# A selective-scan layer: scan rows reordered to (channel, state), state sums in four column groups of one PSUM bank, stores of ACT-made tiles issued from ACT's queue, and the first convolution tap moved to ACT

## The chip, the cores and the metric

The kernel runs on one core of one Trainium2 chip. The metric is the device time of one execution in microseconds (us). Times are medians of four runs (for the kernel before, of three when it was first profiled).

## The reference, cut to what matters

The layer takes x of shape (8, 384, 32, 32): eight images of 1024 tokens and 384 channels. In float32 throughout:

```python
xz = layernorm(t) @ in_proj_w.T ; xm, z = split(xz)          # 768 inner channels
xc = silu(causal_conv3(xm))                                   # three taps per channel
dt, B, C = split(xc @ x_proj_w.T) ; dt = softplus(dt @ dt_proj_w.T + b)
h[t] = exp(dt[t] * A) * h[t-1] + dt[t] * xc[t] * B[t]          # 768 channels x 16 states
y[t] = sum over the 16 states of h[t] * C[t]  +  xc[t] * D
t = gelu((y * silu(z)) @ out_proj_w.T @ mlp_w1.T + b) @ mlp_w2.T + b ; x = x + t
x = x + ffn(norm(x))                                           # two projections with binarised weights
```

The scan over 768 x 16 independent rows of 1024 tokens is the core. For each image it takes 96 tiles of 128 rows.

## The kernel before

A tile of 128 rows is 32 channels by 4 states. Its work is a ring over four engines: an exponential on ACT, a product on GpSimd, the scan and a product with C on DVE, and a sum over the states on TensorE (a matmul with a 128x32 matrix of zeros and ones, `fold`). The projections of the neighbouring images are woven between the tiles; the order on each engine is fixed when the program is built. In the profiles PE is TensorE (PEld its weight loads), DVE is VectorE, ACT is ScalarE, POOL is GpSimd, and SPq and ACTq are the queues from which SP and ACT issue transfers. The parts that matter:

```python
# rows of a tile are (state, channel): partition = state * 32 + channel
def quad_rows(first, q):                      # B or C rows: 4 states, each to 32 partitions
    src = rows[first + q * SQ : first + (q + 1) * SQ, :]
    nc.sync.dma_start(r, src.unsqueeze(1).to_broadcast([SQ, DQ, L]))      # 4 x 32 x 1024
def rep(d, j, name):                          # dt or dt*x: 32 channels, each to 4 states; 3 buffers
    src = d[j * DQ : (j + 1) * DQ, :]
    nc.sync.dma_start(r, src.unsqueeze(0).to_broadcast([SQ, DQ, L]))      # 4 x 32 x 1024
...
def sums(py, pair, q, hcs):                   # py: 128 x 1024, two banks
    for cols in HALVES:
        for jj, hc in zip(pair, hcs):
            nc.tensor.matmul(py[jj * DQ : (jj + 1) * DQ, cols], self.fold, hc[:, cols], ...)
...
for m in range(KD):                           # 6 times 128 channels
    py = ...; xr = (1 buffer) ; zr = (1 buffer)
    for p0 in (0, 2):                         # two tiles at a time
        dts, dtxs = two loads each
        for q in range(NQUAD):
            for i, jj in enumerate(pair):
                da = exp(dts[i] * a)                                      # ACT, into PSUM, 2 buffers
                u = dtxs[i] * b_q[q]                                      # GpSimd
                da = scan(da, u)                                          # DVE
                hc = da * c_q[q]                                          # DVE, 4 buffers
            # the pair's sums are given out one tile later
```

All loads and stores except the constants are issued from SP's queue. The program's PSUM tiles take eight banks: four for da, two for py and two for the projections.

Of the kernel before, what the change touches and what calls it, by code (L numbers as in the profile page):

```python
# [30 lines left out]
P = 128  # L31
# [13 lines left out]
NQUAD = NS // SQ  # L45
NJ = DI // DQ

NUM_GROUPS = 5
# [14 lines left out]
class Layer:  # L63
    def __init__(self, ctx, tc, a, out):
        self.tc, self.nc, self.a, self.out = tc, tc.nc, a, out

        def pool(name, bufs, **kw):
            return ctx.enter_context(tc.tile_pool(name=name, bufs=bufs, **kw))

        self.const = pool("const", 1)  # L70
        self.big = pool("big", 4)
        self.wk = pool("wk", 2)
        self.wt = pool("wt", 4)
        self.small = pool("small", 2)
        self.sc = pool("scan", 2)
        self.bc = pool("bc", 1)
        self.dram = pool("dram", 2, space=DRAM)
        self.dram1 = pool("dram1", 1, space=DRAM)
        self.ps_da = pool("ps_da", 2, space=PSUM)
        self.ps_y = pool("ps_y", 1, space=PSUM)  # L80
        self.ps = pool("ps", 2, space=PSUM)
        self.st = {}
        self.x_mid = [self.dram1.tile([C, L], F32, name=f"x_mid{b}") for b in range(NQ)]
        self.constants()
# [3 lines left out]
    def constants(self):  # L88
# [6 lines left out]
        self.fold = const.tile([P, DQ], F32, name="fold")  # L95
        nc.vector.tensor_add(self.fold, ident[:, :DQ], ident[:, DQ : 2 * DQ])
        for k in range(2, SQ):
            nc.vector.tensor_add(self.fold, self.fold, ident[:, k * DQ : (k + 1) * DQ])
        self.eps_m = const.tile([P, 1], F32, name="eps_m")
# [4 lines left out]
        def vec(name, k):  # L104
# [4 lines left out]
        self.ln_w, self.ln_b, self.mlp_b2 = vec("ln_w", KC), vec("ln_b", KC), vec("mlp_b2", KC)  # L109
        self.conv_b, self.dt_b, self.d_skip = (  # L110
            vec("conv_b", KD), vec("dt_proj_b", KD), vec("D", KD),
        )
        self.mlp_b1 = vec("mlp_b1", KH)
# [57 lines left out]
    def s1(self, b):  # L171
        nc, a = self.nc, self.a
        dt_d = self.dram.tile([DI, L], F32, tag="dt_d", name="dt_d")
        dtx_d = self.dram.tile([DI, L], F32, tag="dtx_d", name="dtx_d")
        xc_d = self.dram.tile([DI, L], F32, tag="xc_d", name="xc_d")
        z_d = self.dram.tile([DI, L], F32, tag="z_d", name="z_d")
        rows = self.dram.tile([2 * NS, L], F32, tag="rows", name="rows")
# [6 lines left out]
        for half, cols in enumerate(HALVES):  # L184
# [11 lines left out]
            for m in range(KD):  # L196
                pm = self.mm3(self.w_cols(a["in_proj_w"][m]), t, "p_in")
                xm = self.wk.tile([P, T + 2], F32, tag="xm", name="xm")
                nc.scalar.copy(xm[:, 2:], pm)  # L199
                if half == 0:  # L200
                    nc.gpsimd.memset(xm[:, :2], 0.0)
                    nc.gpsimd.tensor_copy(halo[:, m, :], xm[:, T:])
                else:
                    nc.gpsimd.tensor_copy(xm[:, :2], halo[:, m, :])
                nc.vector.tensor_scalar(
                    xc[:, m, :], xm[:, :T], self.conv_w[:, m, 0:1],
                    self.conv_b[:, m : m + 1], ALU.mult, ALU.add,
                )
                for j in (1, 2):
                    nc.vector.scalar_tensor_tensor(  # L210
                        xc[:, m, :], xm[:, j : j + T], self.conv_w[:, m, j : j + 1],
                        xc[:, m, :], ALU.mult, ALU.add,
                    )
                yield 3
# [6 lines left out]
            nc.scalar.activation(z, z, AF.Silu)  # L221
            nc.sync.dma_start(tiled(xc_d, cols), xc)
            nc.sync.dma_start(tiled(z_d, cols), z)

# [7 lines left out]
            nc.scalar.copy(dbc, p_dbc)  # L232
            nc.sync.dma_start(rows[:, cols], dbc[R:, :])
            yield 6
# [10 lines left out]
            nc.scalar.activation(dt, dt, AF.Softplus)  # L245
            nc.sync.dma_start(tiled(dt_d, cols), dt)
            for d in range(KD):
# [6 lines left out]
    def s2(self, b):  # L254
        nc, tc = self.nc, self.tc
        dt_d, dtx_d, xc_d, z_d, rows = self.st[b]
        yg_d = self.dram.tile([DI, L], F32, tag="yg_d", name="yg_d")
        self.st[b] += (yg_d,)

        def quad_rows(first, q):  # L260
            r = self.bc.tile([P, L], F32, tag=f"bc{first}_{q}", name=f"bc{first}_{q}")
            src = rows[first + q * SQ : first + (q + 1) * SQ, :]
            nc.sync.dma_start(r, src.unsqueeze(1).to_broadcast([SQ, DQ, L]))
            return r

        def rep(d, j, name):
            r = self.sc.tile([P, L], F32, tag=name, name=name, bufs=3)
            src = d[j * DQ : (j + 1) * DQ, :]
            nc.sync.dma_start(r, src.unsqueeze(0).to_broadcast([SQ, DQ, L]))
            return r  # L270
# [3 lines left out]

        def sums(py, pair, q, hcs):
            for cols in HALVES:
                for jj, hc in zip(pair, hcs):
                    nc.tensor.matmul(  # L278
                        py[jj * DQ : (jj + 1) * DQ, cols], self.fold, hc[:, cols],
                        start=(q == 0), stop=(q == NQUAD - 1),  # L280
                    )

        def gate(m, py, xr, zr):
# [3 lines left out]
            nc.gpsimd.tensor_mul(xr, xr, zr)  # L287
            nc.sync.dma_start(yg_d[m * P : (m + 1) * P, :], xr)

        for m in range(KD):  # L290
            py = self.ps_y.tile([P, L], F32, tag="y", name="py")
            xr = self.sc.tile([P, L], F32, tag="xr", name="xr", bufs=1)
            zr = self.sc.tile([P, L], F32, tag="zr", name="zr", bufs=1)
            for p0 in (0, 2):
                pair = (p0, p0 + 1)
                dts = [rep(dt_d, m * SQ + jj, "dt_r") for jj in pair]
                dtxs = [rep(dtx_d, m * SQ + jj, "dtx_r") for jj in pair]
                if p0 == 0:
                    nc.sync.dma_start(xr, xc_d[m * P : (m + 1) * P, :])
                    nc.sync.dma_start(zr, z_d[m * P : (m + 1) * P, :])  # L300
                for q in range(NQUAD):
                    if q not in b_q:
                        b_q[q] = quad_rows(0, q)
                        c_q[q] = quad_rows(NS, q)
                    hcs = []
                    for i, jj in enumerate(pair):
                        col = (m * SQ + jj) * NQUAD + q
                        da = self.ps_da.tile([P, L], F32, tag="da", name="da")
                        nc.scalar.activation(  # L309
                            da, dts[i], AF.Exp, scale=self.a_neg[:, col : col + 1]  # L310
                        )
                        u = self.sc.tile([P, L], F32, tag="u", name="u")
                        nc.gpsimd.tensor_mul(u, dtxs[i], b_q[q])  # L313
                        nc.vector.tensor_tensor_scan(da, da, u, 0.0, ALU.mult, ALU.add)  # L314
                        hc = self.sc.tile([P, L], F32, tag="hc", name="hc", bufs=4)
                        nc.vector.tensor_mul(hc, da, c_q[q])  # L316
                        hcs.append(hc)
                        yield
                        if i == 0:
                            for f in late:  # L320
                                f()
                            late.clear()
                    late.append(lambda py=py, pair=pair, q=q, hcs=hcs: sums(py, pair, q, hcs))
            late.append(lambda m=m, py=py, xr=xr, zr=zr: gate(m, py, xr, zr))
# [5 lines left out]
    def s3(self, b):  # L330
        nc, a = self.nc, self.a
        yg_d = self.st[b][5]
        to = self.x_mid[b] if b < NQ else self.out[b]
        for cols in HALVES:
            yg = self.big.tile([P, KD, T], F32, tag="big", name="yg")
            nc.sync.dma_start(yg, yg_d[:, cols].rearrange("(k p) l -> p k l", p=P))
            t2 = self.wk.tile([P, KC, T], F32, tag="t", name="t2")
# [104 lines left out]
    def f1(self, b):  # L442
# [11 lines left out]
        for m in range(KH):  # L454
            w = self.w_cols(self.w1_d[m])
            for h, cols in enumerate(HALVES):
# [5 lines left out]
                )  # L462
                nc.sync.dma_start(y1_d[m, :, cols], y)
                yield 3
# [111 lines left out]
def _laid_out(i):  # L576
# [14 lines left out]
    a = {"x": np.asarray(i["x"]).reshape(B, C, L)}  # L591
    for n in ("ln_w", "ln_b", "conv_w", "conv_b", "dt_proj_b", "D", "mlp_b1", "mlp_b2"):
        a[n] = cols(i[c + n])
    for n in ("x_proj_w", "dt_proj_w"):
        a[n] = np.asarray(i[c + n]).T
    for n in ("in_proj_w", "out_proj_w", "mlp_w1"):
        a[n] = blocks(i[c + n])
    w2 = blocks(i[c + "mlp_w2"])
    a["mlp_w2"] = w2.reshape(KC, P, 2, HK, P).swapaxes(1, 2)

    al = np.asarray(i[c + "A_log"]).reshape(NJ, DQ, NQUAD, SQ)
    a["A_log"] = al.transpose(3, 1, 0, 2).reshape(P, NJ * NQUAD)
    for n in ("W1", "W2"):
# [22 lines left out]
```

## Time and profile before

| | before |
|---|---|
| median, lowest, highest of three runs | 5466.58, 5451.86, 5474.68 us |
| PE busy | 3987.9 us, 73% |
| DVE, GpSimd, ACT busy | 62%, 39%, 35% |
| DMA busy, mean of 16 engines | 41.5% |

The chain is the work that ended last, followed back from the end of the run through what released each step; "issue" is time for which the profile shows no wait. Here are its shares of the whole span by engine (it was followed back over the last 54% only), then the groups of the scan ring and of the convolution taps: line, engine, operation, operands, count, then busy us and mean ns of one, then idle time before it.

```profile
PE 21%; DMA 15%; DVE 7%; issue 4%; POOL 3%; ACT 2%; SPq 0%; POOLq 0%; DVEq 0%; ACTq 0%
...
L313 POOL TENSOR_TENSOR u<-dtx_r,bc 128x1024 f32<-128x1024 f32 x768 | 1836.4, 2404 | 2665.5 <-DVE da L314 2211.3
L314 DVE TENSOR_TENSOR_SCAN da<-da,u 128x1024 f32<-128x1024 f32 x768 | 1733.7, 2286 | 684.4 <-ACT da L309 597.0
L316 DVE TENSOR_TENSOR hc<-da,bc 128x1024 f32<-128x1024 f32 x768 | 910.9, 1213 | 631.5 <-PE py L278 604.3
...
L210 DVE SCALAR_TENSOR_TENSOR xc<-xm,conv_w,xc 128x512 f32<-128x512 f32 x192 | 155.0, 821 | 1.9
...
L205 DVE TENSOR_SCALAR xc<-xm,conv_w,v_conv_b 128x512 f32<-128x512 f32 x96 | 113.9, 1186 | 52.7 <-ACT xm L199 51.8 <-POOL xm L204 0.4
```

Every member of the ring spends most of its idle time waiting for another member (DVE for ACT and PE, GpSimd for DVE).

### The profile page before, as it was taken

The numbers are of one execution on the slowest core, as the hardware profiler recorded it, in microseconds if no ns is written. First come the engines' busy times: TensorE is split into PE (matmuls) and PEld (weight loads), VectorE is DVE, ScalarE is ACT, GpSimd is POOL, SyncE is SP. The second block draws the span as 40 slices with busy tenths as digits, with TensorE's granted clock in tenths as the row PEclk, the third lists the DMA queues.
The fourth block names the chain that finished last, engine by engine and source line by source line (L and its number), as shares of the span: only waits on it lengthen the run. The fifth ranks groups of instructions, "written<-read, shape, count | busy, mean of one in ns | idle before, by whom it ended". The sixth has DMA issues, their size and how long they took to land.

```text
span 5473.1 us, 29744 instructions
## 1 busy us (share of the span) xinstructions
PE 3987.9 (73%) x9252; PEld 1397.9 (26%) x9252; DVE 3383.6 (62%) x2345; ACT 1919.2 (35%) x1921; POOL 2112.1 (39%) x1072
## 2 busy tenths in 40 slices
PE   8574478756878758878387884887758777658859
PEld 3110032212322213223032221322213223222314
DVE  2598766774575554775646665466664667547860
ACT  3343233432344224443233531344323353223422
POOL 0365434443343243442434434334243343335530
PEclk8786588877988879989698886998869988778979
DMA  4344344333434434445343443446334355334522
GB/s 158 139 158 151 117 142 136 130 126 131 133 134 161 151 119 130 139 141 168 126 141 108 150 144 112 129 130 196 122 113 146 114 179 149 108 128 145 161 96 89
DMA packets 314545, 745.49 MB, mean 136 GB/s; under 512 B 23804, under 2 KB 92924, under 8 KB 314388
## 3 DMA queue, kind: packets, MB, share of 16 engines
q1 hardware_dynamic: 311984, 743.26, 41.5%
q8 instruction: 74, 1.21, 0.1%
q14 instruction: 83, 0.68, 0.0%
q10 hardware_dynamic: 2404, 0.33, 0.0%
HBM read 560.01 MB, written 183.50 MB: 136 GB/s over the span
## 4 chain that ended last, share of the span: by engine, by line
PE 21%; DMA 15%; DVE 7%; issue 4%; POOL 3%; ACT 2%; SPq 0%; POOLq 0%; DVEq 0%; ACTq 0%
DMA dt_r<-dt_d 6%; PE p_h L143 5%; PE p_o L367 3%; DVE da L314 3%; PE py L278 3%; PE p_out L342 3%; PE p_y L489 2%; PE p_y L143 2%; POOL u L313 2%; DVE hc L316 2%; DMA w<-in_mlp_w 2%; PE p_z L143 1%; DMA y_d<-y 1%; DMA yg_d<-xr 1%; ACT da L309 1%
## 5 line engine op out<-in xcount | busy, mean ns | idle before, releaser
L313 POOL TENSOR_TENSOR u<-dtx_r,bc 128x1024 f32<-128x1024 f32 x768 | 1836.4, 2404 | 2665.5 <-DVE da L314 2211.3
L314 DVE TENSOR_TENSOR_SCAN da<-da,u 128x1024 f32<-128x1024 f32 x768 | 1733.7, 2286 | 684.4 <-ACT da L309 597.0
L278 PE MATMUL py<-hc,fold 128*32 128x512 f32 x3072 | 1047.1, 721 | 744.7 <-DVE hc L316 704.8
L309 ACT ACTIVATE da<-dt_r,a_neg 128x1024 f32<-128x1024 f32 x768 | 853.8, 1116 | 1949.5 <-DVE hc L316 1318.5
L316 DVE TENSOR_TENSOR hc<-da,bc 128x1024 f32<-128x1024 f32 x768 | 910.9, 1213 | 631.5 <-PE py L278 604.3
L143 PE MATMUL p_h<-t,w 128*128 128x512 f32 x1152 | 533.8, 619 | 110.2 <-DMA w<-in_mlp_w 73.5
L278 PEld LDWEIGHTS py<-hc,fold 128*32 128x32 f32 x3072 | 194.1, 120 | 1536.5 <-DVE hc L316 933.5
L367 PE MATMUL p_o<-g,w 128*128 128x512 f32 x1152 | 519.1, 606 | 17.2 <-DMA w<-in_mlp_w 16.2
L143 PE MATMUL p_in<-t,w 128*128 128x512 f32 x576 | 318.9, 711 | 196.7 <-DMA w<-in_in_proj_w 89.0
L143 PE MATMUL p_y<-tn,w 128*128 128x512 f32 x720 | 344.5, 638 | 95.7 <-ACT y L459 72.3
L342 PE MATMUL p_out<-yg,w 128*128 128x512 f32 x576 | 272.1, 631 | 138.1 <-DMA yg<-yg_d 100.1
L489 PE MATMUL p_y<-gf,w 128*128 128x512 f32 x720 | 341.1, 633 | 37.2 <-DMA w<-bin_W 29.3
L143 PEld LDWEIGHTS p_h<-t,w 128*128 128x128 f32 x1152 | 222.5, 197 | 419.6 <-issue 364.7
L143 PE MATMUL p_z<-t,w 128*128 128x512 f32 x576 | 276.0, 631 | 40.6 <-ACT xm L199 15.4
L367 PEld LDWEIGHTS p_o<-g,w 128*128 128x128 f32 x1152 | 217.9, 193 | 318.2 <-issue 297.9
L143 PEld LDWEIGHTS p_in<-t,w 128*128 128x128 f32 x576 | 126.1, 228 | 395.8 <-issue 235.1
L143 PEld LDWEIGHTS p_y<-tn,w 128*128 128x128 f32 x720 | 144.4, 204 | 295.0 <-issue 207.3
L353 ACT ACTIVATE g<-p_h,v_mlp_b 128x512 f32<-128x512 f32 x192 | 129.9, 683 | 252.6 <-PE p_h L143 252.4
L489 PEld LDWEIGHTS p_y<-gf,w 128*128 128x128 f32 x720 | 143.0, 203 | 240.4 <-issue 213.4
L460 DVE TENSOR_REDUCE mx<-y 128x1 f32<-128x512 f32 x120 | 80.5, 676 | 187.2 <-ACT y L459 187.2
L372 DVE SCALAR_TENSOR_TENSOR res<-p_o,v_mlp_b,res 128x512 f32<-128x512 f32 x48 | 35.5, 740 | 256.1 <-PE p_o L367 256.1
L342 PEld LDWEIGHTS p_out<-yg,w 128*128 128x128 f32 x576 | 114.7, 203 | 302.0 <-issue 263.4
(81 smaller groups left out, 2553.7 us busy)
## 6 DMA issues: line engine op xcount, KB each, us to landing
dt_r<-dt_d SPq DMA_DIRECT2D x192, 512.0 KB
dtx_r<-dtx_d SPq DMA_DIRECT2D x192, 512.0 KB
w<-in_in_proj_w SPq DMA_DIRECT2D x192, 192.0 KB
w<-in_mlp_w SPq DMA_DIRECT2D x96, 384.0 KB
w<-in_mlp_w SPq DMA_DIRECT2D x192, 192.0 KB
bc<-rows SPq DMA_DIRECT2D x64, 512.0 KB
y_d<-y SPq DMA_DIRECT2D x120, 256.0 KB
gf<-y_d SPq DMA_DIRECT2D x20, 1536.0 KB
```

The source lines that it names most:

```text
L143: self.nc.tensor.matmul(pm, w[:, k, :], t[:, k, :], start=(k == 0), stop=(k == KC - 1))
L278: nc.tensor.matmul(py[jj * DQ : (jj + 1) * DQ, cols], self.fold, hc[:, cols], start=(q == 0), stop=(q == NQUAD - 1),)
L309: nc.scalar.activation(da, dts[i], AF.Exp, scale=self.a_neg[:, col : col + 1])
L313: nc.gpsimd.tensor_mul(u, dtxs[i], b_q[q])
L314: nc.vector.tensor_tensor_scan(da, da, u, 0.0, ALU.mult, ALU.add)
L316: nc.vector.tensor_mul(hc, da, c_q[q])
L342: nc.tensor.matmul(pm, w[:, k, :], yg[:, k, :], start=(k == 0), stop=(k == KD - 1))
L353: nc.scalar.activation(gh[:, h % HK, :], pm, AF.Identity, bias=self.mlp_b1[:, h : h + 1])
L367: nc.tensor.matmul(po, w[:, k, :], g[i][:, k, :], start=(i + k == 0), stop=(i * HK + k == KH - 1),)
L372: nc.vector.scalar_tensor_tensor(res, po, self.mlp_b2[:, m : m + 1], res, ALU.add, ALU.add)
L460: nc.vector.tensor_reduce(mx[:, m, h : h + 1], y, AX.X, ALU.max, apply_absolute_value=True)
L489: nc.tensor.matmul(pm, w[:, k, :], g[i][:, k, :], start=(i + k == 0), stop=(i * HK + k == KH - 1),)
```

## The change

Its stated intent: order the scan rows as (channel, state); collect an image's state sums for 64 channels and both halves in the four 32-column groups of one bank, which frees a bank for the projections; store the tiles that ACT makes from ACT's own queue; and put the first of three convolution taps on ACT. The core of the diff:

```diff
-        self.ps = pool("ps", 2, space=PSUM)
+        self.ps = pool("ps", 3, space=PSUM)
...                                          # fold and A's host layout follow the new row order
-                nc.vector.tensor_scalar(
-                    xc[:, m, :], xm[:, :T], self.conv_w[:, m, 0:1],
-                    self.conv_b[:, m : m + 1], ALU.mult, ALU.add,
+                nc.scalar.activation(
+                    xc[:, m, :], xm[:, :T], AF.Identity,
+                    bias=self.conv_b[:, m : m + 1], scale=self.conv_w[:, m, 0:1],
                 )
...                                          # xc, z, rows, dt and y1 stores: nc.sync -> nc.scalar
-            nc.sync.dma_start(r, src.unsqueeze(1).to_broadcast([SQ, DQ, L]))
+            nc.sync.dma_start(r, src.unsqueeze(0).to_broadcast([DQ, SQ, L]))
...
-            nc.sync.dma_start(r, src.unsqueeze(0).to_broadcast([SQ, DQ, L]))
+            nc.sync.dma_start(r, src.unsqueeze(1).to_broadcast([DQ, SQ, L]))
...
-        def sums(py, pair, q, hcs):
-            for cols in HALVES:
-                for jj, hc in zip(pair, hcs):
+        def sums(py, q, hcs):
+            for jj, hc in enumerate(hcs):
+                for h, cols in enumerate(HALVES):
+                    p0 = h * DP + jj * DQ
                     nc.tensor.matmul(
-                        py[jj * DQ : (jj + 1) * DQ, cols], self.fold, hc[:, cols],
+                        py[p0 : p0 + DQ, :], self.fold, hc[:, cols],
...
-            py = self.ps_y.tile([P, L], F32, tag="y", name="py")
-            xr = self.sc.tile([P, L], F32, tag="xr", name="xr", bufs=1)
-            zr = self.sc.tile([P, L], F32, tag="zr", name="zr", bufs=1)
+            py = self.ps_y.tile([P, T], F32, tag="y", name="py")
+            xr = self.sc.tile([P, T], F32, tag="xr", name="xr")
+            zr = self.sc.tile([P, T], F32, tag="zr", name="zr")
```

The last lines carry two changes that the title does not name: xr and zr are halved and get two buffers each, and the gate (y + D xc, times silu(z)) runs 12 times an image on 128x512 instead of 6 times on 128x1024.

More of the change, by code (lines that the diff above doesn't have):

```diff
@@ L46 @@
 NJ = DI // DQ
+DP = 2 * DQ
+NP = DI // DP
 NUM_GROUPS = 5
@@ L95, in constants @@
         self.fold = const.tile([P, DQ], F32, name="fold")
-        nc.vector.tensor_add(self.fold, ident[:, :DQ], ident[:, DQ : 2 * DQ])
-        for k in range(2, SQ):
-            nc.vector.tensor_add(self.fold, self.fold, ident[:, k * DQ : (k + 1) * DQ])
+        nc.vector.tensor_reduce(
+            self.fold, ident.rearrange("p (d n) -> p d n", n=SQ), AX.X, ALU.add
+        )
         self.eps_m = const.tile([P, 1], F32, name="eps_m")
@@ L109, in constants @@
         self.ln_w, self.ln_b, self.mlp_b2 = vec("ln_w", KC), vec("ln_b", KC), vec("mlp_b2", KC)
-        self.conv_b, self.dt_b, self.d_skip = (
-            vec("conv_b", KD), vec("dt_proj_b", KD), vec("D", KD),
-        )
+        self.conv_b, self.dt_b = vec("conv_b", KD), vec("dt_proj_b", KD)
+        self.d_skip = vec("D", NP)
         self.mlp_b1 = vec("mlp_b1", KH)
@@ L174, in s1 @@
         dtx_d = self.dram.tile([DI, L], F32, tag="dtx_d", name="dtx_d")
-        xc_d = self.dram.tile([DI, L], F32, tag="xc_d", name="xc_d")
-        z_d = self.dram.tile([DI, L], F32, tag="z_d", name="z_d")
+        xc_d = self.dram.tile([NP, P, T], F32, tag="xc_d", name="xc_d")
+        z_d = self.dram.tile([NP, P, T], F32, tag="z_d", name="z_d")
         rows = self.dram.tile([2 * NS, L], F32, tag="rows", name="rows")
@@ L221, in s1 @@
             nc.scalar.activation(z, z, AF.Silu)
-            nc.sync.dma_start(tiled(xc_d, cols), xc)
-            nc.sync.dma_start(tiled(z_d, cols), z)
+            for d, t_ in ((xc_d, xc), (z_d, z)):
+                for i in range(2):
+                    to = d[i::2, half * DP : (half + 1) * DP, :].rearrange("k p l -> p k l")
+                    nc.scalar.dma_start(to, t_[i * DP : (i + 1) * DP, :, :])
             p_dbc = self.ps.tile([R + 2 * NS, T], F32, tag="mm", name="p_dbc")
@@ L232, in s1 @@
             nc.scalar.copy(dbc, p_dbc)
-            nc.sync.dma_start(rows[:, cols], dbc[R:, :])
+            nc.scalar.dma_start(rows[:, cols], dbc[R:, :])
             yield 6
@@ L245, in s1 @@
             nc.scalar.activation(dt, dt, AF.Softplus)
-            nc.sync.dma_start(tiled(dt_d, cols), dt)
+            nc.scalar.dma_start(tiled(dt_d, cols), dt)
             for d in range(KD):
@@ L256, in s2 @@
         dt_d, dtx_d, xc_d, z_d, rows = self.st[b]
-        yg_d = self.dram.tile([DI, L], F32, tag="yg_d", name="yg_d")
+        yg_d = self.dram.tile([NP, P, T], F32, tag="yg_d", name="yg_d")
         self.st[b] += (yg_d,)
@@ L287, in gate @@
             nc.gpsimd.tensor_mul(xr, xr, zr)
-            nc.sync.dma_start(yg_d[m * P : (m + 1) * P, :], xr)
-        for m in range(KD):
-            py = self.ps_y.tile([P, L], F32, tag="y", name="py")
-            xr = self.sc.tile([P, L], F32, tag="xr", name="xr", bufs=1)
-            zr = self.sc.tile([P, L], F32, tag="zr", name="zr", bufs=1)
-            for p0 in (0, 2):
-                pair = (p0, p0 + 1)
-                dts = [rep(dt_d, m * SQ + jj, "dt_r") for jj in pair]
-                dtxs = [rep(dtx_d, m * SQ + jj, "dtx_r") for jj in pair]
-                if p0 == 0:
-                    nc.sync.dma_start(xr, xc_d[m * P : (m + 1) * P, :])
-                    nc.sync.dma_start(zr, z_d[m * P : (m + 1) * P, :])
-                for q in range(NQUAD):
-                    if q not in b_q:
-                        b_q[q] = quad_rows(0, q)
-                        c_q[q] = quad_rows(NS, q)
-                    hcs = []
-                    for i, jj in enumerate(pair):
-                        col = (m * SQ + jj) * NQUAD + q
-                        da = self.ps_da.tile([P, L], F32, tag="da", name="da")
-                        nc.scalar.activation(
-                            da, dts[i], AF.Exp, scale=self.a_neg[:, col : col + 1]
-                        )
-                        u = self.sc.tile([P, L], F32, tag="u", name="u")
-                        nc.gpsimd.tensor_mul(u, dtxs[i], b_q[q])
-                        nc.vector.tensor_tensor_scan(da, da, u, 0.0, ALU.mult, ALU.add)
-                        hc = self.sc.tile([P, L], F32, tag="hc", name="hc", bufs=4)
-                        nc.vector.tensor_mul(hc, da, c_q[q])
-                        hcs.append(hc)
-                        yield
-                        if i == 0:
-                            for f in late:
-                                f()
-                            late.clear()
-                    late.append(lambda py=py, pair=pair, q=q, hcs=hcs: sums(py, pair, q, hcs))
@@ new lines, in gate @@
+            nc.sync.dma_start(yg_d[m], xr)
+        for m in range(NP):
+            py = self.ps_y.tile([P, T], F32, tag="y", name="py")
+            xr = self.sc.tile([P, T], F32, tag="xr", name="xr")
+            zr = self.sc.tile([P, T], F32, tag="zr", name="zr")
+            dts = [rep(dt_d, m * 2 + jj, "dt_r") for jj in range(2)]
+            dtxs = [rep(dtx_d, m * 2 + jj, "dtx_r") for jj in range(2)]
+            nc.sync.dma_start(xr, xc_d[m])
+            nc.sync.dma_start(zr, z_d[m])
+            for q in range(NQUAD):
+                if q not in b_q:
+                    b_q[q] = quad_rows(0, q)
+                    c_q[q] = quad_rows(NS, q)
+                hcs = []
+                for jj in range(2):
+                    col = (m * 2 + jj) * NQUAD + q
+                    da = self.ps_da.tile([P, L], F32, tag="da", name="da")
+                    nc.scalar.activation(
+                        da, dts[jj], AF.Exp, scale=self.a_neg[:, col : col + 1]
+                    )
+                    u = self.sc.tile([P, L], F32, tag="u", name="u")
+                    nc.gpsimd.tensor_mul(u, dtxs[jj], b_q[q])
+                    nc.vector.tensor_tensor_scan(da, da, u, 0.0, ALU.mult, ALU.add)
+                    hc = self.sc.tile([P, L], F32, tag="hc", name="hc", bufs=4)
+                    nc.vector.tensor_mul(hc, da, c_q[q])
+                    hcs.append(hc)
+                    yield
+                    if jj == 0:
+                        for f in late:
+                            f()
+                        late.clear()
+                late.append(lambda py=py, q=q, hcs=hcs: sums(py, q, hcs))
@@ L333, in s3 @@
         to = self.x_mid[b] if b < NQ else self.out[b]
-        for cols in HALVES:
+        for half, cols in enumerate(HALVES):
             yg = self.big.tile([P, KD, T], F32, tag="big", name="yg")
-            nc.sync.dma_start(yg, yg_d[:, cols].rearrange("(k p) l -> p k l", p=P))
+            for i in range(2):
+                src = yg_d[i::2, half * DP : (half + 1) * DP, :].rearrange("k p l -> p k l")
+                nc.sync.dma_start(yg[i * DP : (i + 1) * DP, :, :], src)
             t2 = self.wk.tile([P, KC, T], F32, tag="t", name="t2")
@@ L462, in f1 @@
                 )
-                nc.sync.dma_start(y1_d[m, :, cols], y)
+                nc.scalar.dma_start(y1_d[m, :, cols], y)
                 yield 3
@@ L591, in _laid_out @@
     a = {"x": np.asarray(i["x"]).reshape(B, C, L)}
-    for n in ("ln_w", "ln_b", "conv_w", "conv_b", "dt_proj_b", "D", "mlp_b1", "mlp_b2"):
+    for n in ("ln_w", "ln_b", "conv_w", "conv_b", "dt_proj_b", "mlp_b1", "mlp_b2"):
         a[n] = cols(i[c + n])
@@ L597, in _laid_out @@
         a[n] = blocks(i[c + n])
+    a["D"] = np.tile(np.asarray(i[c + "D"]).reshape(NP, DP).T, (2, 1))
     w2 = blocks(i[c + "mlp_w2"])
@@ L601, in _laid_out @@
     al = np.asarray(i[c + "A_log"]).reshape(NJ, DQ, NQUAD, SQ)
-    a["A_log"] = al.transpose(3, 1, 0, 2).reshape(P, NJ * NQUAD)
+    a["A_log"] = al.transpose(1, 3, 0, 2).reshape(P, NJ * NQUAD)
     for n in ("W1", "W2"):
```

## The prediction

> **What bounds the kernel now.** I read the page's engine totals first, then the same totals stage by stage, then the waits, then the chain that ended last, and at last the DMA rate inside its longest pieces.
>
> ```profile
> PE 3987.9 (73%) x9252; PEld 1397.9 (26%) x9252; DVE 3383.6 (62%) x2345; ACT 1919.2 (35%) x1921; POOL 2112.1 (39%) x1072
> ...
> L278 PE MATMUL py<-hc,fold 128*32 128x512 f32 x3072 | 1047.1, 721 | 744.7 <-DVE hc L316 704.8
> L309 ACT ACTIVATE da<-dt_r,a_neg 128x1024 f32<-128x1024 f32 x768 | 853.8, 1116 | 1949.5 <-DVE hc L316 1318.5
> ```
>
> TensorE is the busiest engine at 3988 us, and still idles 1485 us of 5473. The eight scans (first scan of one image to first scan of the next) give the windows:
>
> ```profile
> 179.00:661.00 482.00, 270.15 (x576) 64.04 (x576) 418.08 (x315) 173.78 (x164) 266.64 (x132) 0.72 0.42 141
> ...
> 1968.00:2687.00 719.00, 542.81 (x1273) 195.44 (x1272) 435.90 (x304) 255.87 (x258) 261.21 (x134) 0.87 0.42 140
> ```
>
> After the length come PE, PEld, DVE, ACT, POOL busy, the clock, the DMA share and GB/s. The first image is close to bound by DVE (418 of 482); a middle one is bound by no engine (PE 543, DVE 436 of 719). So waits matter, and they form one ring: each tile goes ACT exponential, DVE scan, DVE product, PE sum, and PE takes its sums between the projection matmuls in a fixed order.
>
> ```profile
> PE py L278 <- DVE hc L316: 704.8, 148, 19.0
> ACT da L309 <- DMA dt_r<-dt_d: 615.6, 68, 23.5
> POOL u L313 <- DMA dtx_r<-dtx_d: 355.5, 60, 25.4
> SPq L299 <- DMA yg_d<-xr: 242.5, 44, 15.0
> SPq L300 <- POOL xr L287: 202.7, 33, 17.7
> ```
>
> PE waits mostly for the scan; the scan's own ring has an outside cause, the loads of dt_r and dtx_r: 128 waits, 971 us. The chain shows what they weigh. It was followed back only to 2523 us, so it covers the last 2950 us. Summed by name there: PE work about 1160 us, DMA about 830 (28%), DVE 400, "issue" 244, POOL 150, ACT 105. Of the 830, dt_r is 329 and dtx_r 56, the weights (three names) 207, y_d 71, yg_d 65, gf 61, yg 30. Three pieces, with the rate inside the first:
>
> ```profile
> 2591.74 18.58 DMA dt_r<-dt_d
> ...
> 2644.29 16.47 DMA dt_r<-dt_d
> ...
> 2682.23 23.96 DMA dt_r<-dt_d
> ```
> ```profile
> 2592.00:2600.00 8.00, 8.00 (x21) 3.28 (x21) 4.86 (x3) 1.52 (x2) 4.65 (x2) 1.00 0.26 90
> ```
>
> A 512 KB load takes 16 to 24 us while the DMA share is 0.26 and the rate 90 GB/s. A share of 0.26 is four engines of sixteen. The queue is not full: it is narrow.
>
> **What the skill says.** (1) "DMA: Bandwidth & Descriptors", section "Why a DMA increments its semaphore by 16 and not by 1": the number of DMA engines that a copy runs on is the largest one up to 16 that divides the slowest dimension of both access patterns, and for these queues the lowest-numbered engines are taken. The source of dt_r, dtx_r and the bc rows is laid out as 4 x 32 x 1024, slowest dimension 4, hence four engines, always the same four. The 0.26 agrees. (2) "TensorE: Matmul & The Clock Gate", section "Part 3: Packing small matmuls": matmuls on different column tiles run together, started about 4 ns apart. The trace agrees with two groups: in the timeline around 3050 us, a lone sum matmul (an fp32 matmul is recorded as two) and two sums in two column groups take the same time:
>
> ```profile
> 3050.11 1.05 PE L278 MATMUL py<-hc,fold 128*32 128x512 f32 x4
> ...
> 3067.42 1.04 PE L278 MATMUL py<-hc,fold 128*32 128x512 f32 x2 [1.79 <-DVE hc L316]
> ```
>
> (3) "ScalarE: Activation LUTs", section "What ACT_TABLE_LOAD costs": an ACTIVATE with a pointer bias takes about 280 + 0.833 N ns, and each further pointer operand about 93 more, so about 800 ns for N = 512 with scale and bias; the trace's same form (the layer-norm affine, 128x512) has 802. (4) The DMA page again, "Issuing engines are not separate DMA queues": a second issuing queue saves only the sequencer's time, since the same 16 engines do the work. The before kernel issues nothing but constants from ACT, so nothing here tests that yet.
>
> **The change, part by part.**
> *Row order.* With (channel, state) the sources are 32 x 4 x 1024, slowest dimension 32, so all 16 engines for 448 copies of 512 KB (192 + 192 + 64), 235 MB of the 745 MB moved. A 4096-byte packet takes 160 ns by the packet times. Four engines take 32 packets each, 5.1 us of bare transfer per copy, and the four copies that feed each eight tiles take 20 us; sixteen take 8 packets, 1.3 us, and 5 us for the four. As a check that has the fixed latency in it: the 1.5 MB load of yg, on 16 engines already, is on the chain with 7.4 us. I take a dt_r or dtx_r piece as 5 us in place of 17: 385 us of chain become about 110, 275 saved. Other transfers stop queueing behind those four engines (a weight load's piece is 17 to 20 us for 192 to 384 KB): of the 450 us of other DMA on the chain I take a bit under half, 210.
> *Sums.* Before, an image's pair of tiles uses two column groups: first halves together, then second halves, two rounds of about 2 x 0.43 us, and where the order puts the first of the four matmuls on its own (47 rows of three beside 152 of four in the instruction order) a third round. After, the four go to four groups: one round when they stand together (160 rows of four), two when an early matmul pair stands alone (56 rows of two). About 0.86 us saved per pair, or 1.7 where it was split; for 384 pairs that is 330 to 650 of the 1047 busy us, I take 480. Only where PE is on the path does it count: the sums are 154 us of the chain, half is 80.
> *First tap on ACT.* DVE loses 96 x 1186 ns = 114 us; ACT gains 96 x 802 = 77 us, with over 3500 us idle. DVE's chain has 22 us of it. Price: ACT now waits for GpSimd's two halo columns before the tap, in order, with the next exponentials behind it.
> *Gate in halves.* 96 of 128x512 for 48 of 128x1024: DVE 96 x 740 (the L372 form) - 48 x 1274 = +10 us, GpSimd 96 x 1365 - 48 x 2385 = +17 us. Hidden.
> *Stores from ACT, two buffers for xr and zr.* 96 + 120 issues (six a half image of 16, and y1) at about 0.37 us each, as SP's records have them, put 80 us on ACT's queue. In exchange SP no longer stops for the y1 store (236 us of its waits), nor for xr and zr, which had one buffer (243 + 203 us). These waits hold back the loads behind them; worth on the chain mostly what I have already counted as yg_d, y_d and slow loads: I add 20.
> *A third projection bank* comes free from py; it softens PE's waits for ACT evictions. I count nothing.
>
> Sum on the chain: 275 + 210 + 80 + 22 + 20 = 607 of 2950, 20.6%. Spread over the span that is 1125 us, 4340. But a shortened chain meets the next one: per stage, I set a floor. The first scan stage: DVE 418 less 14 for the taps is 404, so not under about 435 (482 now). The second: PE 407 - 60, DVE 383 - 12, so about 450 (577). A middle stage: PE 543 - 60 = 483, DVE 436 - 12 = 424, with stalls in the proportion of about 1.2 in place of 1.32: 580 (724, four of these). The lighter fifth 525 (661), the last 430 (501); head and tail 170 and 177 (179 each). Sum 435 + 450 + 2320 + 525 + 430 + 347 = 4507. I take 4500.
>
> **Rivals.**
> *The ring stays, only the cause moves.* If dt_r waits are mostly the third buffer's doing (a pair needs two tiles, so the second load can be issued only when the old tile is released), the loads stay late and only get shorter; PE's 705 us of waiting for the scan would fall by less than half. For it: the loads are issued just before they are needed. Against: 18.58 us from issue to landing is transfer, not release. Time about 4850.
> *ACT becomes the in-order bottleneck.* The taps wait for GpSimd, which itself waits 2211 us for the scan; stores wait at ACT's head. For it: ACT serves exponentials, evictions and stores from one queue. Against: 35% busy, and the halo waits of DVE today are 0.4 us. It would cost some 100 to 250 us: 4600 to 4750.
> *PE dense everywhere.* If waits nearly vanish, the floor is PE, 3988 - 480 = 3510, plus head and the DVE-bound first stage, near 3750. Against it: order is fixed at build time, so tiles and fillers don't fit each other that well. I allow 4200.
> *DMA hidden anyway.* If the loads were covered by other work, the row order gives nothing and only the sums count: 5250. The chain's 28% speaks against it.
>
> **Range and chances.** From 4200 (DMA almost gone) to 4850 (first rival). Faster by over 2% at 0.97; within 2% at 0.02; slower 0.01.
>
> **What would show it.** The dt_r and dtx_r waits of ACT and GpSimd together under 350 us; no long window at a DMA share of 0.25; the py row near 550 us busy; PE's wait for hc under 450; the TENSOR_SCALAR row gone from DVE, an 0.8 us row x96 on ACT. I'm wrong if dt_r pieces of over 12 us remain on the chain, if the py row stays near 1000 (groups not running four at a time), or if ACT waiting for GpSimd or for DMA takes the place of the old waits.

## The result, and the profile after

The changed kernel took 4610.67 us (median of 4 runs, 4606.61 to 4616.37) against 5459.37 for the kernel before (5451.86 to 5474.68; a fourth run has joined the three above). The ratio is 0.8443, 95% interval 0.842 to 0.8467.

From the page of the changed kernel: engine totals, the chain by engine, the sums and the exponentials, and the loads with their median time from issue to landing.

```profile
PE 3626.6 (79%) x9252; PEld 1289.4 (28%) x9252; DVE 3330.3 (72%) x2295; ACT 2003.7 (43%) x2025; POOL 2135.0 (46%) x1120
...
PE 43%; DVE 27%; issue 13%; ACT 7%; DMA 3%; POOL 3%; ACTq 0%; DVEq 0%; SPq 0%; POOLq 0%
...
L311 ACT ACTIVATE da<-dt_r,a_neg 128x1024 f32<-128x1024 f32 x768 | 855.4, 1116 | 1406.6 <-DVE hc L318 1347.6
L283 PE MATMUL py<-hc,fold 128*32 128x512 f32 x3072 | 745.1, 749 | 650.5 <-DVE hc L318 583.6
...
dt_r<-dt_d SPq DMA_DIRECT2D x192, 512.0 KB, 5.1
dtx_r<-dtx_d SPq DMA_DIRECT2D x192, 512.0 KB, 4.0
```

A load of dt_r lands in 5.1 us where the three pieces of before took 16 to 24. DMA was 830 of the 2950 us that the chain of before covered (28%); now it is 3% of the span. The chain is no longer about transfers: PE has 43% and DVE, which had 13.6% of the covered chain, has 27%.

The waits of the changed kernel that answer to those of before (who waits, for whom, us in total, times, longest):

```profile
PE py L283 <- DVE hc L318: 583.6, 160, 14.5
...
POOL u L315 <- DMA dtx_r<-dtx_d: 15.3, 1, 15.3
...
SPq L293 <- POOL xr L292: 611.9, 92, 23.3
...
SPq L301 <- DMA yg_d<-xr: 130.6, 75, 7.4
```
```profile
L311 ACT ACTIVATE da<-dt_r,a_neg 128x1024 f32<-128x1024 f32 x768 | 855.4, 1116 | 1406.6 <-DVE hc L318 1347.6 <-DMA w<-bin_W 18.5 <-DMA dt_r<-dt_d 15.5
```

ACT's wait for dt_r, 615.6 us before, is 15.5 (the last line, from the view that keeps shapes apart), and GpSimd's for dtx_r went from 355.5 to 15.3. SP now stands 612 us at the yg_d store, because the gate runs twice as often; that is a longer wait in front of later loads than the ones removed, and yet transfers are 3% of the chain: a queue that waits costs nothing here, since what it carries lands in time.

Two stages, cut at the first scan of each image as before, and a stretch in which broadcast loads run:

```profile
172.00:613.00 441.00, 250.44 (x594) 59.36 (x593) 414.61 (x309) 184.78 (x178) 272.03 (x137) 0.66 0.49 154
...
1680.00:2288.00 608.00, 499.05 (x1272) 182.85 (x1272) 430.71 (x299) 267.88 (x272) 265.28 (x141) 0.88 0.52 165
```
```profile
2280.00:2300.00 20.00, 7.98 (x20) 0.94 (x20) 18.97 (x13) 5.16 (x5) 14.53 (x7) 0.50 0.77 272
```

In the last line dt_r, dtx_r and bc loads run at a DMA share of 0.77 and 272 GB/s, where a stretch with the same kind of load ran at 0.26 and 90 GB/s before. And the ring is tight there: DVE is busy 18.97 of 20 us.

### The profile page after: what moved, and what is told of

Its sections match the earlier page's. It is cut to its first block, busy times and chain, and to the rows that moved or that the text cites. A ratio compares the mean times of both kernels' runs of the same rounds, so it can differ in the third digit from the quotient of the medians.

```text
span 4606.6 us, 29985 instructions
## 1 busy us (share of the span) xinstructions
PE 3626.6 (79%) x9252; PEld 1289.4 (28%) x9252; DVE 3330.3 (72%) x2295; ACT 2003.7 (43%) x2025; POOL 2135.0 (46%) x1120
## 4 chain that ended last, share of the span: by engine, by line
PE 43%; DVE 27%; issue 13%; ACT 7%; DMA 3%; POOL 3%; ACTq 0%; DVEq 0%; SPq 0%; POOLq 0%
DVE da L316 13%; PE p_h L144 10%; PE p_o L371 9%; DVE hc L318 6%; PE p_y L144 5%; PE p_out L346 5%; ACT da L311 4%; PE py L283 4%; PE p_z L144 3%; PE p_y L493 3%; DVE xc L212 3%; POOL u L315 2%; PE p_dbc L232 1%; PE p_dt L242 1%; DMA gf<-y_d 1%
## 5 line engine op out<-in xcount | busy, mean ns | idle before, releaser
L283 PE MATMUL py<-hc,fold 128*32 128x512 f32 x3072 | 745.1, 749 | 650.5 <-DVE hc L318 583.6
L144 PE MATMUL p_h<-t,w 128*128 128x512 f32 x1152 | 510.3, 598 | 2.8 <-ACT t L349 1.8
L371 PE MATMUL p_o<-g,w 128*128 128x512 f32 x1152 | 509.6, 597 | 2.0 <-ACT g L362 2.0
L283 PEld LDWEIGHTS py<-hc,fold 128*32 128x32 f32 x3072 | 98.9, 118 | 1237.1 <-DVE hc L318 891.2
L144 PE MATMUL p_in<-t,w 128*128 128x512 f32 x576 | 288.9, 661 | 89.5 <-ACT t L191 89.3
L144 PE MATMUL p_y<-tn,w 128*128 128x512 f32 x720 | 328.7, 615 | 26.3 <-DVE tn L168 19.4
L346 PE MATMUL p_out<-yg,w 128*128 128x512 f32 x576 | 259.6, 607 | 10.6 <-issue 10.6
L212 DVE SCALAR_TENSOR_TENSOR xc<-xm,conv_w,xc 128x512 f32<-128x512 f32 x192 | 204.0, 1079 | 33.1 <-ACT xc L207 30.3
L292 POOL TENSOR_TENSOR xr<-xr,zr 128x512 f32<-128x512 f32 x96 | 126.1, 1314 | 155.0 <-DVE xr L289 113.3
```

Of the source, the lines that this page charges most:

```text
L144: self.nc.tensor.matmul(pm, w[:, k, :], t[:, k, :], start=(k == 0), stop=(k == KC - 1))
L212: nc.vector.scalar_tensor_tensor(xc[:, m, :], xm[:, j : j + T], self.conv_w[:, m, j : j + 1], xc[:, m, :], ALU.mult, ALU.add,)
L283: nc.tensor.matmul(py[p0 : p0 + DQ, :], self.fold, hc[:, cols], start=(q == 0), stop=(q == NQUAD - 1),)
L292: nc.gpsimd.tensor_mul(xr, xr, zr)
L346: nc.tensor.matmul(pm, w[:, k, :], yg[:, k, :], start=(k == 0), stop=(k == KD - 1))
L371: nc.tensor.matmul(po, w[:, k, :], g[i][:, k, :], start=(i + k == 0), stop=(i * HK + k == KH - 1),)
```

## The experiments

The predicted time was inside its range, so the question was which part did it, and whether for the reason given. All twelve runs gave correct results, each beside runs of the kernel before on the same chip. Those of before stayed between 5450.86 and 5480.19 us.

One caution goes with the table. An edit can change the order that the builder gives to the instructions of each engine. By the traces, run 1 keeps the order of the kernel before, and run 2 that of the changed kernel, on TensorE, ACT and GpSimd without exception; run 8 keeps it nearly. In the other runs it moved: of the changed kernel's 637 groups of like matmuls at most 519 keep their order in run 7, 568 in run 9 and 486 in run 10. So the differences of 27 to 63 us that these runs show include whatever the new order is worth, which was not tested.

| run | median us | ratio to before (95%) |
|---|---|---|
| changed kernel | 4610.67 | 0.8443 (0.842 to 0.8467) |
| 1 row order alone | 4749.07 | 0.8681 (0.8668 to 0.8695) |
| 2 all but the row order | 5533.78 | 1.0118 (1.0096 to 1.014) |
| 3 old order, four copies per load | 5098.37 | 0.9318 (0.9303 to 0.9333) |
| 4 new order, four copies per load | 5072.18 | 0.9288 (0.9267 to 0.931) |
| 5 new order, four copies, 8 engines | 5124.74 | 0.9377 (0.936 to 0.9394) |
| 6 row order, tap and stores | 4743.59 | 0.8669 (0.8656 to 0.8683) |
| 7 two projection banks | 4673.48 | 0.8559 (0.8543 to 0.8576) |
| 8 one buffer for xr, zr | 4615.21 | 0.8452 (0.8432 to 0.8472) |
| 9 tap back on DVE | 4656.14 | 0.8529 (0.8512 to 0.8546) |
| 10 stores back on SP | 4583.8 | 0.8395 (0.8379 to 0.8411) |
| 11 stores on SP, six hc buffers | 4550.51 | 0.8331 (0.8319 to 0.8343) |
| 12 as 11, sums one pair later | 4596.25 | 0.8415 (0.8403 to 0.8428) |

**1. Row order alone**, on the kernel before:

```diff
-            nc.sync.dma_start(r, src.unsqueeze(0).to_broadcast([SQ, DQ, L]))
+            nc.sync.dma_start(r, src.unsqueeze(1).to_broadcast([DQ, SQ, L]))
...          # the same for the B and C rows; fold and A's layout to match
```

> The kernel before with the row order alone changed (fold matrix, A's layout and the two broadcast loads; two column groups, stores and tap as before). My theory, that the order matters because it spreads the 448 broadcast copies over 16 engines instead of 4: most of the 849 us gain, 4850 to 5000 us; ACT's and GpSimd's waits for dt_r and dtx_r from 971 us to under 150; py row still near 1050 us busy. Rival A, the column groups and the shorter PE order carry the gain: 5250 or more. Rival B, the loads stay late because of the third buffer: waits for dt_r and dtx_r over 450 us and a time over 5150.

It took 4749.07 us: 725 us less than the 5473.65 of its own rounds, of 849 for the whole change. The sums' row of this run (its page) has the old busy time and a shorter idle time, and the waits for the loads are nearly gone:

```profile
L278 PE MATMUL py<-hc,fold 128*32 128x512 f32 x3072 | 1061.5, 730 | 565.9 <-DVE hc L316 540.0
...
ACT da L309 <- DMA dt_r<-dt_d: 32.1, 6, 8.4
...
POOL u L313 <- DMA dtx_r<-dtx_d: 10.3, 1, 10.3
```

The waits for dt_r and dtx_r, the last two lines, were 32.1 and 10.3 us. The row order carries the gain, by more than the 4850 to 5000 us that I had expected. Rivals A and B are out: the third buffer was never the limit once a load took 5 us.

**2. All but the row order**: the reverse edit, on the changed kernel.

> The changed kernel with the old (state, channel) row order and its four-engine loads, all else changed. My theory: most of the gain is lost, 5150 to 5350 us, with dt_r pieces of 15 us and more back on the chain and ACT's plus GpSimd's waits for them over 700 us. Rival A: stays under 4850.

It took 5533.78 us, worse than the kernel before by 1.2%. ACT's wait for dt_r in this run, from the list of waits, and the chain by engine, from its page:

```profile
ACT da L311 <- DMA dt_r<-dt_d: 775.6, 80, 43.5
```
```profile
DMA 31%; PE 30%; DVE 15%; issue 8%; ACT 6%; POOL 5%; SPq 1%; ACTq 0%; DVEq 0%; POOLq 0%
```

With the narrow loads left in, four column groups, a third bank, a lighter DVE and a second queue buy nothing. I had expected them to keep 120 to 320 us of the gain; they lost 60. The parts do not add up: the others are worth -60 us without the row order and +138 us (4749 to 4611) with it.

**3, 4 and 5. Number of engines, or order of reading?** The new order changes two things in a broadcast load: its slowest dimension (4 to 32), and that a DRAM row is read four times in a row rather than once in each of four passes (for dt and dt*x; for the B and C rows it is the old order that re-reads a row at once). Run 3 keeps the old order and widens the load by issuing four copies of 32 partitions:

```diff
-            nc.sync.dma_start(r, src.unsqueeze(0).to_broadcast([SQ, DQ, L]))
+            for n in range(SQ):
+                nc.sync.dma_start(r[n * DQ : (n + 1) * DQ, :], src)
...          # B and C rows likewise
```

> The kernel before with its old (state, channel) order, but each broadcast load issued as four copies of 32 partitions, so that the slowest dimension is 32 and all 16 engines carry it. Price: 1344 more issues on SP, some 0.35 us each, 470 us of SP's time, mostly idle time. If the number of engines is the cause: within 3% of the run with the row order alone, and no window at a DMA share of 0.25. If it is the order in which DRAM rows are read again (the same row four times in a row): near 5459 us, as before.

It took 5098.37 us: 375 us of run 1's 725, matching neither expectation. So I put the same four-copy form on the new order (run 4, four copies to every fourth partition), and then one with rows re-read at once but only eight channels to a copy, so a slowest dimension of 8 (run 5):

```diff
-            nc.sync.dma_start(r, src.unsqueeze(1).to_broadcast([DQ, SQ, L]))
+            for n in range(SQ):                                   # run 4
+                nc.sync.dma_start(r[n::SQ, :], src)
+            for g in range(4):                                    # run 5
+                s = src[g * 8 : (g + 1) * 8, :].unsqueeze(1).to_broadcast([8, SQ, L])
+                nc.sync.dma_start(r[g * DQ : (g + 1) * DQ, :], s)
```

> The row-order-alone kernel (4749 us) with every broadcast load issued as four copies, one for each state, to every fourth partition: new row order, 16 engines, but 1344 more issues and each DRAM row read again only four copies later, as in the old-order run with four copies (5098 us). If the 5098 came from the four-copy form: 5000 to 5150 us here too. If the row order itself is worth something beyond the number of engines: 4750 to 4850.

> The row-order-alone kernel (4749 us) with every broadcast load issued as four copies, one for each eight channels: the same 1344 extra issues as the two four-copy runs (5098 and 5072 us), but each DRAM row read four times in a row, and a slowest dimension of 8, so 8 engines. If the extra issues cost the 330 us: 5000 us or more here too. If it was the scattered reading of the DRAM rows: 4750 to 4850 us.

Runs 3 and 4, which differ in the row order alone and have the same built order on TensorE, ACT and GpSimd, differ by 0.5% (5098 and 5072 us). So the row order has next to no worth of its own, and what run 1 gained over the kernel before, with an unchanged built order, is due to the number of engines. The four-copy form, with the order that was built for it, has a price of some 320 us (4749 to 5072). Run 5, which reads each row of dt and dt*x four times in a row, pays that price too (5124.74), so scattered reading is not it. A wait that rose, in the list of waits of run 3:

```profile
POOL u L317 <- DMA dtx_r<-dtx_d: 501.2, 55, 24.4
```

The loads land quickly (3.3 us median for a piece), but the four issues of one dtx_r load take 8.9 us from first to last on average, other issues and their waits standing between them, against 0.5 us for the one issue. GpSimd waits for the last piece, and DVE for GpSimd: its wait for the product u is 449 us in run 4 against 51 in run 1. That this is the whole price is argued, not tested, and there is a rival: runs 3, 4 and 5 share one built order, but it is not that of run 1. Of TensorE's 659 groups of like matmuls at most 437 keep their order. The two causes were not told apart.

The number of engines was read off the packet records of the traces, by counting the packets in flight at each moment. The time spent at one count:

```
packets in flight     4        8        16
before             1940 us    58 us    609 us
changed kernel       47       67       948
2 (all but order)  1945       65       700
5 (dimension 8)      90      767       604
```

A slowest dimension of 4, 8 or 32 gives a heap at 4, 8 or 16 packets. For 1940 us of its time the kernel before had four of sixteen engines at work. The new order with four engines in one issue, which would separate the two directly, was not run.

**6, 7 and 8. The four groups, the third bank, the second buffer.** Run 6 is the kernel before with row order, tap and stores changed. Runs 7 and 8 are one-line edits of the changed kernel:

```diff
-        self.ps = pool("ps", 3, space=PSUM)
+        self.ps = pool("ps", 2, space=PSUM)                                   # run 7
-            xr = self.sc.tile([P, T], F32, tag="xr", name="xr")
+            xr = self.sc.tile([P, T], F32, tag="xr", name="xr", bufs=1)       # run 8, zr too
```

> The changed kernel without the four column groups: row order, tap on ACT and stores from ACT's queue, but py in two banks with two groups, gate and xr/zr whole with one buffer, and two projection banks. My theory: 4700 to 4800 us (the sums worth 2 to 4%), py row near 1000 us busy. Rival, the sums are off the path: within 1% of 4611 us. Rival A, they carry it: over 5000.

> The changed kernel with two projection banks instead of three. The four groups and the third bank together are worth 133 us (4744 to 4611). If the third bank is what carries it: 4700 us or more, PE's waits for evictions by ACT up by over 60 us. If the four groups carry it: under 4650.

> The changed kernel with one buffer each for xr and zr instead of two. Of the 133 us between the run without the four groups (4744) and the changed kernel (4611), the third bank carries 62 (4673 without it); this asks how much of the other 71 is the second buffer and how much is left for the four groups themselves. My theory, the second buffer is off the path now that loads are short: 4611 to 4640 us, SP waiting longer for the yg_d store and the gate. Rival: 4670 us or more, the four groups worth almost nothing.

Run 6 took 4743.59 us, as I had expected, with the sums' row at 1066.1 us busy. So four groups, third bank, halved gate and second buffer together are worth 133 us. Without the third bank alone the time is 4673.48, 63 us more than with it; PE waits there more for ACT's evictions (ACT copying a projection out of its PSUM bank), from run 7's list of waits:

```profile
PE p_in L144 <- ACT xm L201: 53.3, 24, 3.5
```

The changed kernel has no such row. All of PE's waits for evictions together rose from 56 to 116 us, the 60 that I had expected; but its wait for the layer norm's t fell from 89 to 40, so that PE idled only 27 us more in all and was busy 36 us longer. My expectation for run 7 had asked for 4700 us to call the bank the carrier, and under 4650 for the groups: it fell between, and both count. The second buffer is worth 5 us, within noise, although SP's waits for xr and zr were 446 us before. What is left for the four groups with the halved gate is about 65 us, by difference and not by a run of their own.

**9. First tap back on DVE.**

> The changed kernel with the first conv tap back on DVE. The run without the four column groups (4744 us) and the one with the row order alone (4749 us) say that tap and stores together are worth nothing. My theory: DVE busy up by 65 us, not 114 (the profile shows that the stretch that a GpSimd product puts on a DVE instruction moved to the next tap); time 4600 to 4650 us, the same within 1%. Rival, DVE is on the path now and the tap counts in full: 4675 us or more.

It took 4656.14 us, 45 more than the changed kernel: the tap is worth 1.0%, just outside what I had expected and below the rival's 4675. DVE busy rose by 59 us (3330.3 to 3389.7), not by the 114 of the row that was removed.

**10. Stores back on SP.**

> The changed kernel with the ACT-made tiles stored from SP's queue again. My theory: within 1% of 4611 us; SP's waits for ACT's tiles return (some 250 us), ACT's y1 wait changes little. Rival 1, SP as the head-of-line blocker counts: 4680 or more. Rival 2, the issues in ACT's queue hurt: under 4560.

It took 4583.8 us, 27 less: with those stores on ACT the kernel is 0.6% slower. The SP waits for ACT's tiles do return (147 us for y1 alone). What they replace is 216 issues with 115 us of ACT's queue time, the 16 stores of the B and C rows taking 2.4 us each in the median. That these issues are what costs the 27 us is argued; the built order moved as well.

**11 and 12. Two tries to beat both.** Both keep the stores on SP and have six hc buffers; run 12 also gives the sums out one pair of tiles later.

```diff
-                    hc = self.sc.tile([P, L], F32, tag="hc", name="hc", bufs=4)
+                    hc = self.sc.tile([P, L], F32, tag="hc", name="hc", bufs=6)
...
-                        for f in late:
+                        for f in older:                       # run 12 only
                             f()
+                        older[:] = late
                         late.clear()
```

> Try to beat both: the changed kernel with the stores back on SP (4584 us) and six hc buffers instead of four. DVE waits 386 us for PE to free an hc buffer. If that wait is on the path, 4480 to 4540 us with the wait under 200 us; if PE's waits only move along with it, within 1% of 4584.

> As the run with six hc buffers and SP stores, and the sums given out one pair of tiles later, so that PE meets them when hc is long ready. PE waits 584 us for hc in the changed kernel. If deferral makes them ready: that wait under 300 us and 4400 to 4530 us. If the two extra buffers are used up by the delay: near 4584 us.

Run 11 took 4550.51 us, 1.3% faster than the changed kernel and the best of all. DVE's wait for PE to release hc, in each of the two runs:

```profile
DVE hc L318 <- PE py L283: 296.0, 71, 20.4
```
```profile
DVE hc L318 <- PE py L283: 437.0, 76, 29.2
```

It was 386 in the changed kernel and 415 in run 10, on which both build. Two more buffers took 119 us off that; deferring the sums brought it back to 437. PE's wait for hc, 622 in run 10, is 550 and 541. The second of my two expectations for each run is nearest, with a gain of 0.7% from the buffers.

## Why the prediction was right or wrong

**The time, right**: 4610.67 predicted as 4500, range 4200 to 4850. The sum by stages can be laid beside the measured stages:

| stage | predicted | measured |
|---|---|---|
| head | 170 | 172 |
| first image | 435 | 441 |
| second | 450 | 459 |
| four middle images | 4 x 580 | 608, 608, 613, 614 |
| fifth | 525 | 527 |
| last | 430 | 391 |
| tail | 177 | 174 |

The miss is in the middle images, 123 us in all; the last image gave 39 back. There I had set PE to 543 - 60 = 483 and DVE to 424; measured are 499 and 431. The factor of 1.2 held (608 / 499 = 1.22). It was the floors by stage that brought the number near: the sum on the chain alone had given 4340. And part of it is luck: the third bank's 63 us were left out and the stores were put at +37 where they measured -27, two errors that cancel.

**Row order, right in mechanism, somewhat too large in size.** I took 485 us off 2950 us of chain, 16%. Run 1 measures 13.2% of the whole time; DMA fell further than I had put it (28% to 3% of the chain), but DVE and "issue" took its place, as the stage floors had foreseen. That four engines were the cause is shown by run 1, which keeps the built order, by runs 3 and 4, where the row order alone is worth 0.5%, and by the packet counts: the Trainium skill's rule of the slowest dimension, as cited in the prediction, agrees with 4, 8 and 16.

**Sums, mis-sized.** I took 480 us of PE busy time; 302 came (1047 to 745). The mechanism is in the timeline of the changed kernel (start, length, line): in the second line eight records, four sums in four groups, take the time that four records took before.

```profile
401.30 1.92 PE L283 MATMUL py<-hc,fold 128*32 128x512 f32 x4 [1.76 <-DVE hc L318]
...
2022.50 1.06 PE L283 MATMUL py<-hc,fold 128*32 128x512 f32 x8
```

The low end of the estimate, 330 us, was near. What failed is the 1.7 us for a pair that is split: by the traces such a pair took 1.05 + 1.90 us before (two records, then six) and takes 1.05 + 1.05 now (four and four), 0.85 less, no more than a pair that stands together (1.91 to 1.07). The first line shows a second loss. Where PE has less to do its granted clock is lower (0.66 in the first image, where it is busy 250 of 441 us, and 0.88 in a middle one, busy 499 of 608; 0.56 in the stretch from 400 to 425 us; each clock record of the trace has 1.0 or 0.5), so that four records take 1.92 us instead of 1.05, and eight some 3.05: 69 of the 139 bursts of four records and 80 of the 249 of eight are so slow (records less than 0.1 us apart make a burst). Of the 3072 records, 963 start at half clock, 818 before. The Trainium skill's page "TensorE: Matmul & The Clock Gate", section "Part 1: The HAM clock gate (the "warmup" mystery)", tells of a half-speed state after idling, and this agrees: 1.92 / 1.05 = 1.8. The slow bursts are most frequent in the first image, where PE has time to spare; a middle image got 41 us (128.6 to 87.6) of the 60 I had put down.

**Third bank: "I count nothing" was wrong.** It measures 63 us, as much as the four groups with the halved gate, built order included.

**First tap: right in time, wrong in busy time.** The chain had 22 of 2950 us for it, so 41 of the span; run 9 gives 45. That is in part luck, since the 22 us belong to a saving of 114 us of busy time that did not come: DVE's taps lost 65 us and not 114 (268.9 to 204.0). The remaining taps became slower on average (821 to 1079 ns); the tap on ACT takes 812:

```profile
L207 ACT ACTIVATE xc<-xm,v_conv_b,conv_w 128x512 f32<-128x512 f32 x96 | 77.9, 812 | 44.3 <-POOL xm L203 22.3 <-POOL xm L206 16.6
...
L212 DVE SCALAR_TENSOR_TENSOR xc<-xm,conv_w,xc 128x512 f32<-128x512 f32 x192 | 204.0, 1079 | 33.1 <-ACT xc L207 30.3
```

Instruction by instruction, taps that run beside a GpSimd product last 1.48 us on average and all others at most 0.753; a stretched one ends mostly 0.55 us after the GpSimd product does (0.28 for the first tap, before). The Trainium skill's page "SBUF — State Buffer", section "SBUF: two separate sides", describes an exclusive lock on the port pair that DVE and GpSimd share, held for a whole instruction; this agrees. It fits that the first tap of a block met the lock, and that the next one met it when the first was taken away: with the first tap back on DVE in run 9, the others average 838 ns again.

**Stores and second buffer: wrong in sign and size.** I added 20 us of chain, 37 of the span. With the stores on ACT the kernel is 27 us slower, and the buffer is worth 5. The Trainium skill's page "DMA: Bandwidth & Descriptors", section "Issuing engines are not separate DMA queues", says that a second issuer saves only the sequencer's time; run 10 agrees: the second issuer brought no gain.

**The rivals.** The third buffer as the true limit (4850) is refuted by waits of 31 us, though its sign came true: PE's wait for the scan fell by less than half, from 705 to 584. ACT as the bottleneck had 4600 to 4750, and the measured time lies in it, but its cause came true in a small part only: ACT waits 39 us for GpSimd's halo columns, and the stores measure 27. My signs for "right" were met for dt_r waits (31, under 350) and the new ACT row (812 ns, 0.8 us expected); missed for the py row (745, not 550) and PE's wait for hc (584, not under 450): PE still waits for DVE, whose share of the span rose from 62% to 72%.

## What to carry to other kernels

When a load is slow, look first at the DMA share and the rate inside its wait: here a share of 0.26 meant that four of sixteen engines carried it, and the shape of the source, the outermost dimension of a broadcast, was worth more than any buffer or second queue. Splitting a load into more issues widened it too, but here that form, with 1344 more issues and another built order, gave back some 320 us. As long as the narrow transfers were there, the improvements elsewhere in the same ring measured as a loss of 60 us; without them, as a gain of 138. And before a difference of 1% is put down to an edit, compare the built orders.

## What the Trainium skill lacked or had wrong

- "DMA: Bandwidth & Descriptors" has no figure for what the extra issues of a split load cost in a queue that other issues share. Here four copies for one made the time from first to last issue of a dtx_r load 8.9 us on average in a busy SP queue, against 0.5 us, and the kernel, with the order built for it, 320 us slower.
- "TensorE: Matmul & The Clock Gate", section "Part 3: Packing small matmuls": its measured table has no case of four column tiles alone, and names no number type. Here four fp32 sums of 128x512 in four groups take 1.06 us, one alone 1.04, and two in two groups 1.05; the sums of one burst start 6 to 7 ns apart, where the page has about 4.
